# A two-layer decoder on one core: the products of a packed set held together on TensorE, and early work tied to its group's transpose

## The chip, the core and the metric

The kernel runs on one core of one Trainium2 chip. The metric is the time of one execution on the device in microseconds (us); the median of several executions counts. Everything is computed in 32-bit floats. The engines are called as the profile calls them: PE is TensorE's matrix multiplication and PEld its loading of weights, DVE is VectorE, ACT is ScalarE, POOL is GpSimd, and SP is the queue that issues nearly all loads and stores.

## The reference, cut to what matters

The input x is 16 sequences of 128 tokens with 256 features. Two decoder layers follow each other. Each has an attention, a cross stage and a feed-forward stage, and after each stage comes a layer norm of x plus the stage's result:

```python
x = _layernorm(x + _L0_attn_ref(x, ...))   # 16 heads of 64, causal
x = _layernorm(x + _L0_xattn_ref(x, ctx_512, itok, proj_in, proj_out))  # 8 experts, gates
x = _layernorm(x + _L0_ffn_ref(x, ...))    # 2 shared and 16 routed experts, the best 2 taken
x = _layernorm(x + _L1_attn_ref(x, ...))   # 16 heads of 16, a band of 8 to either side
x = _layernorm(x + _L1_xattn_ref(x, ctx_512, ctx_512, ...))  # 16 heads of 16
x = _layernorm(x + _L1_ffn_ref(x, ...))    # 8 experts, scaled by a gate
```

In the second stage the gate of expert e for a token sums `ctx_512` over the places k at which `itok` names e:

```python
onehot = jax.nn.one_hot(ensembles, E, dtype=x.dtype)
gate = jnp.einsum('bks,bkse->bse', weights, onehot)
return jnp.einsum('bsei,bse->bsi', o, gate)
```

So the gates depend on inputs of the kernel alone, and not on x. Neither do the expert weights.

## The kernel before

The 16 sequences form 4 groups of 4, so that a group is 512 tokens. A stage of a group is a Python generator that writes a few instructions and then yields. A planner (`Weaver`, line 193) takes turns between a main chain of stages, a side chain ("dense") and short jobs, by guessed costs and due times. The chains are set at the end (lines 1018 to 1028): first the attention of groups 0 and 1 of layer 0 alone, then that of groups 2 and 3 with dense stages beside it, then the two attentions of layer 1 for all groups with dense stages beside them, and last the dense rest.

This order of writing is not yet the order on the engines. The framework's scheduler takes instructions for each engine by priority, which is the order of writing, among those that it believes ready. So an instruction that was written late but needs little can stand early in its engine's queue. Each engine then runs its own queue strictly in order and waits for semaphores at its head.

**Packed products.** Four kinds of product use only part of the 128x128 array, and are written in sets whose members lie on different parts of it:
- The scores of the attention of layer 0 (line 389): four products for a pair of heads twice, with 64 rows each, from rows 0 and 64.
- Its values (line 432): four products with 64 columns each.
- The scores of the attentions of layer 1 (line 473): two products with 64 rows each and 512 columns of output, one to each of two banks.
- Their values (line 485): four products with 32 columns each.

A fifth kind is the gates' sums (line 751): four products with 32 columns each. Between the members of a set the scheduler may put other products. The other matrix work, projections (292), values' projections (309), hidden layers and the experts' second products (670), uses the whole array. A 32-bit product is two passes in the trace; a transpose (line 51) is one.

**PSUM.** The accumulators are banks of the tags H (projections), M (experts), O (transposes and values), with two buffers each, and S (scores), with one. A projection into H has to wait until DVE or ACT has copied out the one before the last.

**Gates.** `gates0(g)` loads `it` and `cx` into single buffers. Four comparisons on DVE (line 742) give four products `chose`, PE sums each over its partitions, ACT copies the sums, and SP stores them to HBM; then the same for the other four experts. `gates0(g)` is written right after the group's activations were transposed behind its first attention (`tail`, line 951). The transpose consists of eight products on PE and two copies, one on DVE (247) and one on ACT (249). The ACT copy is kept in `transposed_by[g]`. Nothing binds the comparisons to it.

**Expert weights.** The second weights of an expert are needed as seven blocks and their differences. `load_blocks` makes them on POOL when an expert is used first: four subtractions (line 632) and three copies (636), of which only the subtraction of block 4 is bound to the group's transpose. The blocks are stored to HBM and loaded again for the other groups. `together(first, *steps)` is the helper for such a binding: it makes one instruction wait for others.

The sums of the hidden layer's parts (658 to 661), which the experts' second products need, are on DVE.

Of the kernel before, what the change touches and what calls it, by code (L numbers as in the profile page):

```python
# [1 line left out]

# [12 lines left out]
P = 128  # L15
# [12 lines left out]
def kernel(ctx: ExitStack, tc: tile.TileContext, a: dict, out: bass.AP):  # L28
    nc = tc.nc
# [17 lines left out]
    mm = nc.tensor.matmul  # L47

    def transpose(out_, in_):
        n = in_.shape[0]  # L50
        return nc.tensor.transpose(out_, in_, ident[:n, :n])  # L51

    def together(first, *steps):

        for step in steps:
            tc.add_manual_dep(
                first.ins, step.ins.name,
                mybir.DependencyInfo(mybir.DependencyClass.Sync, mybir.DependencyReason.DATA),
                reason="together",
            )  # L60
# [291 lines left out]
    heads0 = {}  # L352

    def attention0(x, g):
        norm = Norm(x)
        norm.bias(bo0)

        def project_quad(g, j):
            wq, wk, wv, wo = first_quads[j] if g == 0 and j < 2 else load_quad(j)
            xT = xTs[g]  # L360
            qT = p2.tile([P, 2, T], F32, tag="qT", name="qT")
            kT = p2.tile([P, 2, T], F32, tag="kT", name="kT")
            for i in range(2):
                c = 2 * j + i
                cols = slice(i * P, (i + 1) * P)
                pq = bank("H")
                project(pq, wq, cols, xT)
                nc.vector.tensor_scalar(
                    qT[:, i, :], pq, bq0[:, c:c + 1], 0.125, ALU.add, ALU.mult
                )  # L370
                pk = bank("H")
                project(pk, wk, cols, xT)
                nc.scalar.activation(kT[:, i, :], pk, AF.Identity, bias=bk0[:, c:c + 1])
                yield 3.44

            v = yield from values(xT, wv, KC)
            heads0[g, j] = qT, kT, v, wo

        def scores(j, b):
            qT, kT, _, _ = heads0[g, j]  # L380
            at = slice(b * P, (b + 1) * P)
            s = ps.tile([P, 2, T], F32, tag="S", name="psS", bufs=1)[:, :, :D].rearrange(
                "p s (i k) -> p s i k", i=2
            )

            for i in range(2):
                for k in range(2):
                    rows = slice(64 * k, 64 * k + 64)
                    mm(  # L389
                        s[:, k, i, :], lhsT=qT[rows, i, at], rhs=kT[rows, i, at],  # L390
                        start=True, stop=True,
                    )
            return softmax(s, causal)

        def output(j, b, zT):
            po = bank("H")[:, :D]
            for i in range(2):
                mm(po, lhsT=zT[:, i, :], rhs=heads0[g, j][3][:, i, :], start=i == 0, stop=i == 1)  # L398
            norm.add(b, po, last=j == 3)

        if (g, 0) not in heads0:
            yield from project_quad(g, 0)
        units = [(j, b) for j in range(4) for b in range(GB)]
        e, eT, zT, at = {}, {}, {}, {}
        for n in range(len(units) + 5):
            if n < 16:
                j, b = units[n]
                e[n] = scores(j, b)
                at["e", n] = weaver.now + 9.0
                yield 0.6  # L410
            m = n - 2
            if m in e:
                yield UNTIL, at["e", m]
                eT[m], _ = weights_T(e.pop(m))
                at["t", m] = weaver.now + 2.5
                yield 0.5
            m = n - 5
            if m in zT:
                yield UNTIL, at["z", m]
                output(*units[m], zT.pop(m))  # L420
                yield 0.86
            m = n - 4
            if m in eT:
                j, b = units[m]
                yield UNTIL, at["t", m]

                pz = bank("O")[:, :D].rearrange("p (c q) -> p c q", c=2)
                got = eT.pop(m)
                for i in range(2):
                    for k in range(2):  # L430
                        h = 2 * i + k
                        mm(  # L432
                            pz[64 * k:64 * k + 64, i, :],
                            lhsT=heads0[g, j][2][:, b, 64 * h:64 * h + 64], rhs=got[:, 2 * k + i, :],
                            start=True, stop=True,
                        )
                zT[m] = p3.tile([P, 2, P], F32, tag="z", name="zT")

                nc.vector.tensor_tensor(
                    zT[m], pz, bv0[:, 2 * j:2 * j + 2].unsqueeze(2).to_broadcast([P, 2, P]), ALU.add  # L440
                )
                at["z", m] = weaver.now + 2.5
                yield 0.6
            if n < 16 and (n < 12 or g + 1 < NG):

                j, b = units[n]
                if b == 0:
                    ahead = project_quad(g, j + 1) if j < 3 else project_quad(g + 1, 0)
                yield next(ahead)
                if b == 3:  # L450
                    assert next(ahead, None) is None
        assert not e and not eT and not zT
        norm.done()


    def attention16(x, qT, kT, v, bv, wo, bo, seen):
# [3 lines left out]
        def scores(b, c):  # L460

            at = slice(b * P, (b + 1) * P)

            kb = p2.tile([P, 4, P], F32, tag="kb", name="kb")
            nc.gpsimd.tensor_tensor(  # L465
                kb, kT[:, c, at].unsqueeze(1).to_broadcast([P, 4, P]),
                hm4.unsqueeze(2).to_broadcast([P, 4, P]), ALU.mult,
            )
            yield UNTIL, weaver.now + 2.0
            s = ps.tile([P, 2, T], F32, tag="S", name="psS", bufs=1)  # L470
            for k in range(2):
                rows = slice(64 * k, 64 * k + 64)
                mm(  # L473
                    s[:, k, :], lhsT=qT[rows, c, at], rhs=kb[rows].rearrange("p h k -> p (h k)"),
                    start=True, stop=True,
                )
            return softmax(s.rearrange("p s (h k) -> p s h k", h=4), seen)

        def weigh(b, c, eT):


            pz = bank("O")[:, :D].rearrange("p (k q) -> p k q", k=2)
            for r in range(4):
                rows = slice(32 * r, 32 * r + 32)
                step = mm(  # L485
                    pz[rows], lhsT=v[:, b, c * P + 32 * r:c * P + 32 * r + 32],
                    rhs=eT[r // 2][0][:, 2 * (r % 2):2 * (r % 2) + 2, :],
                    start=True, stop=True,
                )
                if r == 0:  # L490
                    together(step, eT[1][1])
            if c == 0:
                zT[b] = p3.tile([P, 2, P], F32, tag="z", name="zT16")
            half_z = p2.tile([P, P], F32, tag="hz", name="hz")
            if bv is None:
                nc.scalar.activation(half_z, pz[:, 0, :], AF.Copy, scale=even[:, 0:1])
            else:
                nc.scalar.activation(
                    half_z, pz[:, 0, :], AF.Identity, scale=even[:, 0:1], bias=bv[:, c:c + 1]
                )  # L500
            nc.vector.scalar_tensor_tensor(  # L501
                out=zT[b][:, c, :], in0=pz[:, 1, :], scalar=even[:, 1:2], in1=half_z,
                op0=ALU.mult, op1=ALU.add,
            )
# [8 lines left out]
        e, eT, zT, at = {}, {}, {}, {}  # L513
        for n in range(len(units) + 5):
# [5 lines left out]
            if m in e:  # L520
                yield UNTIL, at["e", m]
                got = e.pop(m)
# [94 lines left out]
    transposed_by = {}  # L617

    def load_blocks(layer, e, g, w):
# [10 lines left out]
        minus = [(4, b01, b00), (5, b11, blocks[:, 4]), (2, blocks[:, 5], b10), (3, b11, b01)]  # L630
        for s, one, two in minus:
            step = nc.gpsimd.tensor_tensor(blocks[:, s], one, two, ALU.subtract)
            if s == 4:
                together(step, *transposed_by[g])
        for s, one in ((0, b00), (1, b10), (6, b11)):
            nc.gpsimd.tensor_copy(blocks[:, s], one)
        held = dp.tile([P, 7, 2 * P], F32, tag=f"wb{layer}", name="wbd", bufs=8)
        nc.gpsimd.dma_start(out=held, in_=t)
        in_hbm[layer, e] = held
# [90 lines left out]
    def gates0(g):  # L730
# [7 lines left out]
        for q in range(2):  # L738
            chose = []
            for r in range(4):  # L740
                t = p4.tile([P, T], F32, tag="cw", name="chose")
                nc.vector.scalar_tensor_tensor(
                    out=t, in0=it.rearrange("p b s -> p (b s)"), scalar=float(4 * q + r), in1=cx,
                    op0=ALU.is_equal, op1=ALU.mult,
                )
                chose.append(t)
            yield UNTIL, weaver.now + 3.5

# [349 lines left out]
```

## Time and profile before

| | |
|---|---|
| three timed executions | 1845.22, 1847.55, 1848.01 us; median 1847.55 |
| the profiled execution's own time | 1843.18 us |
| its span, first to last instruction | 1841.5 us |
| mean granted clock of TensorE | 0.989 |
| DVE | 1017.5 us busy |
| gates' comparisons (742) | 32 of 724 ns, 22.3 us busy |
| differences and copies of blocks (632, 636) on POOL | 64 of 722 to 956 ns, 48 of 434 ns |
| loads of function tables on ACT | 1.283 us each |

The profile is read as follows. A row of a group names line, engine, operation, and the tile written and those read, with the number of times, the busy time and the mean duration. A row of the waits names who waited for whom: microseconds in all, times, and the longest. A row of the timeline begins with start and duration in us, and ends with the engine's idle time before it and what ended it. A row of the windows gives for a stretch of the span its length, the busy time of PE, PEld, DVE, ACT and POOL with the number of instructions, the granted clock of TensorE (1.00 is full), the share of the DMA engines' time and GB/s. Matmuls overlap, and their ends are modelled. So the distance from a start to the next start says more than a duration.

### The profile page before, as it was taken

What the parts mean: (1) busy time and instruction counts of PE and PEld (TensorE: products, weight loads), DVE (VectorE), ACT (ScalarE), POOL (GpSimd) and SP (SyncE); (2) the same over time, 40 slices, a digit from 0 to 9 for tenths busy, and PEclk for the clock granted to TensorE, in tenths of its full rate; (3) what the DMA queues carried; (4) which work ended last, traced back from release to release, by engine and by line L of the source; (5) the groups of instructions that cost most, each with busy time, mean ns of one, the idle gap of its engine ahead of it and who ended that gap; (6) DMA issues with size and microseconds to landing.
All of it is one profiled execution on the core that took longest, in us unless ns stands there. A gap on an engine that the chain in (4) does not pass through costs nothing.

```text
span 1841.5 us, 21636 instructions
## 1 busy us (share of the span) xinstructions
PE 1770.8 (96%) x7620; PEld 1074.5 (58%) x7620; DVE 1017.5 (55%) x1983; ACT 724.2 (39%) x2155; POOL 476.1 (26%) x456
## 2 busy tenths in 40 slices
PE   7999999999999999999999989999998999999997
PEld 4665656666566665565565655544655656556665
DVE  3565566576665244875867644346446455545534
ACT  3444321111123441523404437449466276394121
POOL 4232124310002222413303224253552031230000
PEclk8999999999999999999999999999999999999998
DMA  5032223432321333132233222221322112211321
GB/s 170 27 96 80 69 81 119 145 97 98 121 86 60 99 100 124 64 128 80 75 109 112 66 83 73 92 94 64 126 91 84 63 63 85 85 60 67 136 96 52
DMA packets 73468, 166.70 MB, mean 91 GB/s; under 512 B 7064, under 2 KB 38864, under 8 KB 73360
## 3 DMA queue, kind: packets, MB, share of 16 engines
q1 hardware_dynamic: 70528, 150.17, 24.9%
q0 software_dynamic: 2832, 15.15, 2.0%
q8 instruction: 61, 1.00, 0.2%
q14 instruction: 47, 0.39, 0.1%
HBM read 148.32 MB, written 16.97 MB: 90 GB/s over the span
## 4 chain that ended last, share of the span: by engine, by line
PE 78%; DVE 7%; ACT 7%; DMA 3%; POOL 2%; issue 2%; SPq 0%; POOLq 0%; DVEq 0%; ACTq 0%
PE psH L292 34%; PE psM L670 19%; PE psH L309 4%; PE psO L51 4%; ACT e L333 4%; PE psM L600 3%; PE psH L398 3%; PE psS L473 2%; PE psS L389 2%; PE psO L432 2%; PE psO L485 1%; PE psH L51 1%; DVE nmax L328 1%; ACT L333 1%; DMA wquad<-in_L_attn_W_Q 1%
## 5 line engine op out<-in xcount | busy, mean ns | idle before, releaser
L292 PE MATMUL psH<-xT,we 128*128 128x512 f32 x1024 | 490.7, 601 | 4.7 <-ACT h L934 2.6
L339 POOL TENSOR_TENSOR e<-e,inv 128x512 f32<-128x512 f32 (+1 forms) x128 | 191.3, 1495 | 544.8 <-DVE inv L338 498.2
L292 PEld LDWEIGHTS psH<-xT,we 128*128 128x128 f32 x1024 | 187.8, 191 | 168.1 <-issue 138.8
L333 ACT ACTIVATE e<-e,nmax 128x128 f32<-128x128 f32 x512 | 198.6, 389 | 201.6 <-DVE nmax L328 171.6
L670 PE MATMUL psM<-cm,wb 128*128 128x256 f32 x1024 | 267.1, 385 | 1.3 <-DVE acc L682 1.3
L670 PEld LDWEIGHTS psM<-cm,wb 128*128 128x128 f32 x1024 | 191.8, 191 | 69.5 <-issue 44.5
L682 DVE TENSOR_TENSOR acc<-psM,acc 128x512 f32<-128x512 f32 (+1 forms) x216 | 135.6, 628 | 168.6 <-PE psM L670 167.9
L670 PE MATMUL psM<-h,wb 128*128 128x256 f32 x768 | 202.9, 387 | 0.0
L348 ACT COPY eT<-psO 128x512 f32<-128x512 f32 x192 | 106.8, 587 | 228.3 <-PE psO L51 227.6
L670 PEld LDWEIGHTS psM<-h,wb 128*128 128x128 f32 x768 | 142.9, 192 | 56.1 <-issue 35.5
L934 ACT ACTIVATE h<-psH,b 128x512 f32<-128x512 f32 x128 | 87.3, 688 | 221.1 <-PE psH L292 220.6
L292 PE MATMUL psH<-xT,wquad 128*128 128x512 f32 x256 | 121.1, 615 | 13.0 <-DVE v L313 8.5
L773 DVE SCALAR_TENSOR_TENSOR h<-psH,gt 128x512 f32<-128x512 f32 x128 | 87.6, 686 | 73.2 <-PE psH L292 72.7
L51 PEld LDWEIGHTS psO<-ident,e 128*128 128x128 f32 x768 | 87.7, 141 | 51.2 <-issue 34.7
L292 PE MATMUL psH<-xT,wg 128*128 128x512 f32 x256 | 116.3, 595 | 1.1 <-DVE v L313 1.1
L51 PE MATMUL psO<-ident,e 128*128 128x128 f32 x768 | 112.8, 279 | 1.9 <-DVE zT L501 1.6
L465 POOL TENSOR_TENSOR kb<-kT,hm 128x512 f32<-128x512 f32 x64 | 69.3, 1084 | 153.0 <-PE psS L473 93.4
L333 ACT ACTIVATE e<-psS,nmax 128x128 f32<-128x128 f32 x256 | 89.9, 377 | 33.1 <-DVE nmax L328 26.6
L333 ACT ACTIVATION_READ_ACCUMULATOR e<-e,nmax 128x1 f32 x512 | 95.7, 187 | 0.0
L473 PE MATMUL psS<-kb,qT 64*128 64x512 f32 x256 | 82.0, 644 | 14.1 <-ACT e L333 5.0
L292 PEld LDWEIGHTS psH<-xT,wquad 128*128 128x128 f32 x256 | 47.5, 194 | 67.2 <-issue 47.2
L328 DVE TENSOR_REDUCE nmax<-e 128x4 f32<-128x512 f32 (+1 forms) x96 | 82.5, 859 | 2.0
(179 smaller groups left out, 2277.8 us busy)
## 6 DMA issues: line engine op xcount, KB each, us to landing
wb<-wbd SPq DMA_DIRECT2D x48, 896.0 KB
we<-in_L_xattn_proj_in SPq DMA_DIRECT2D x32, 512.0 KB
we<-in_L_ffn_w SPq DMA_DIRECT2D x32, 512.0 KB
wbd<-wb POOLq DMA_DIRECT2D x16, 896.0 KB, 6.1
gt<-gatesd SPq DMA_DIRECT2D x32, 256.0 KB
cw<-combd SPq DMA_DIRECT2D x64, 128.0 KB
wquad<-in_L_attn_W_Q SPq DMA_DIRECT2D x16, 256.0 KB
wquad<-in_L_attn_W_K SPq DMA_DIRECT2D x16, 256.0 KB
```

What stands on the lines that cost most here:

```text
L51: return nc.tensor.transpose(out_, in_, ident[:n, :n])
L292: mm(pt, lhsT=w[:, c, cols], rhs=xT[:, c, :], start=c == 0, stop=c == KC - 1)
L309: mm(pv[:, i, :], lhsT=xT[:, c, (b + i) * P:(b + i + 1) * P], rhs=w[:, c, :], start=c == 0, stop=c == k - 1,)
L328: nc.vector.tensor_reduce(nmax.rearrange("p (s h) -> p s h", s=2), s, AX.X, ALU.max, negate=True)
L333: nc.scalar.activation(e[:, h, :], s[:, h // (n // 2), h % (n // 2), :], AF.Exp, bias=nmax[:, h:h + 1], accum_out=total[:, h:h + 1],)
L339: nc.gpsimd.tensor_tensor(e, e, inv.unsqueeze(2).to_broadcast([P, n, P]), ALU.mult)
L348: return eT, nc.scalar.copy(eT, pt)
L473: mm(s[:, k, :], lhsT=qT[rows, c, at], rhs=kb[rows].rearrange("p h k -> p (h k)"), start=True, stop=True,)
L670: step = mm(pm[:, s % 2, :], lhsT=blocks[e][:, s, q, :], rhs=parts[e][s][:, q, :], start=q == 0 and s % 2 == 0, stop=q == 1, skip_group_ch ...
L682: nc.vector.tensor_tensor(to, pm[:, :len(slots), :], to, ALU.add)
L773: nc.vector.scalar_tensor_tensor(out=h, in0=ph, scalar=0.0, in1=up[1], op0=ALU.max, op1=ALU.mult)
L934: nc.scalar.activation(h, ph, AF.Gelu, bias=b1[:, 4 * e + c:4 * e + c + 1])
```

## The change

A new helper opens the framework's high-priority context for every product of a set but the first, for the scores and values of both kinds of attention:

```diff
+    def joined(first):
+
+        return nullcontext() if first else tc.high_priority()
...
             for i in range(2):
                 for k in range(2):
                     rows = slice(64 * k, 64 * k + 64)
-                    mm(
-                        s[:, k, i, :], lhsT=qT[rows, i, at], rhs=kT[rows, i, at],
-                        start=True, stop=True,
-                    )
+                    with joined(i == k == 0):
+                        mm(
+                            s[:, k, i, :], lhsT=qT[rows, i, at], rhs=kT[rows, i, at],
+                            start=True, stop=True,
+                        )
```

The same is done with `joined(h == 0)` for the values at line 432, `joined(k == 0)` for the scores at 473 and `joined(r == 0)` for the values at 485. The gates' sums at 751 are left as they are.

All seven instructions that make an expert's blocks, and not one alone, are bound to the group's transpose, and so are the gates' comparisons:

```diff
         for s, one, two in minus:
             step = nc.gpsimd.tensor_tensor(blocks[:, s], one, two, ALU.subtract)
-            if s == 4:
-                together(step, *transposed_by[g])
+            together(step, *transposed_by[g])
         for s, one in ((0, b00), (1, b10), (6, b11)):
-            nc.gpsimd.tensor_copy(blocks[:, s], one)
+            together(nc.gpsimd.tensor_copy(blocks[:, s], one), *transposed_by[g])
...
-                nc.vector.scalar_tensor_tensor(
+                step = nc.vector.scalar_tensor_tensor(
                     out=t, in0=it.rearrange("p b s -> p (b s)"), scalar=float(4 * q + r), in1=cx,
                     op0=ALU.is_equal, op1=ALU.mult,
                 )
+                together(step, *transposed_by[g])
                 chose.append(t)
```

No instruction is moved to another engine: the sums of the hidden layer's parts are on DVE in both kernels, and the differences of the weights' blocks on POOL in both. The number of the program's instructions is the same on every engine but ACT, which has six more loads of function tables.

More of the change, by code (lines that the diff above doesn't have):

```diff
@@ L1 @@
-from contextlib import ExitStack
+from contextlib import ExitStack, nullcontext
 import concourse.bass as bass
@@ L431, in attention0 @@
                         h = 2 * i + k
[L432 to L436, printed above, removed]
+                        with joined(h == 0):
+                            mm(
+                                pz[64 * k:64 * k + 64, i, :],
+                                lhsT=heads0[g, j][2][:, b, 64 * h:64 * h + 64],
+                                rhs=got[:, 2 * k + i, :], start=True, stop=True,
+                            )
                 zT[m] = p3.tile([P, 2, P], F32, tag="z", name="zT")
@@ L472, in scores @@
                 rows = slice(64 * k, 64 * k + 64)
[L473 to L476, printed above, removed]
+                with joined(k == 0):
+                    mm(
+                        s[:, k, :], lhsT=qT[rows, c, at],
+                        rhs=kb[rows].rearrange("p h k -> p (h k)"), start=True, stop=True,
+                    )
             return softmax(s.rearrange("p s (h k) -> p s h k", h=4), seen)
@@ L484, in weigh @@
                 rows = slice(32 * r, 32 * r + 32)
[L485 to L489, printed above, removed]
+                with joined(r == 0):
+                    step = mm(
+                        pz[rows], lhsT=v[:, b, c * P + 32 * r:c * P + 32 * r + 32],
+                        rhs=eT[r // 2][0][:, 2 * (r % 2):2 * (r % 2) + 2, :],
+                        start=True, stop=True,
+                    )
                 if r == 0:
```

## The prediction

> **What bounds the kernel.** Read first: the page's busy shares and its chain.
>
> ```profile
> span 1841.5 us, 21636 instructions
> ...
> PE 1770.8 (96%) x7620; PEld 1074.5 (58%) x7620; DVE 1017.5 (55%) x1983; ACT 724.2 (39%) x2155; POOL 476.1 (26%) x456
> ...
> PE 78%; DVE 7%; ACT 7%; DMA 3%; POOL 2%; issue 2%; SPq 0%; POOLq 0%; DVEq 0%; ACTq 0%
> ```
>
> TensorE is busy for 96% of the span and carries 78% of the chain. So two things count: how long its own work takes, and where it stands still. Second, the waits of PE, longest first.
>
> ```profile
> PE psH L292 <- DVE v L313: 9.6, 2, 8.5
> ...
> PE psS L473 <- ACT e L333: 5.0, 3, 2.3
> ...
> PE psS L473 <- DVE e L323: 2.9, 3, 1.9
> ```
>
> One wait of 8.5 us is by far the longest; the rest is many small ones. Third, the timeline of DVE and of PE around it, and the clock there.
>
> ```profile
> 24.76 0.69 DVE L742 SCALAR_TENSOR_TENSOR chose<-it,cx 128x512 f32<-128x512 int32 x1 [12.23 <-DMA cx<-in_ctx]
> 25.37 0.68 DVE L313 COPY v<-psH 128x512 f32<-128x512 f32 x1
> ...
> 16.84 0.71 PE L389 MATMUL psS<-kT,qT 64*128 64x128 f32 x8
> 26.11 6.57 PE L292 MATMUL psH<-xT,wquad 128*128 128x512 f32 x8 [8.55 <-DVE v L313]
> 32.61 0.71 PE L389 MATMUL psS<-kT,qT 64*128 64x128 f32 x8
> ...
> 26.10:32.60 6.50, 6.49 (x8) 2.52 (x8) 4.61 (x8) 1.65 (x8) 3.05 (x5) 0.55 0.10 41
> ```
>
> A gate of group 0 (L742), whose sums PE makes only after 130 us, heads DVE's queue and waits 12.2 us for the load of cx. Behind it stands the copy that frees PE's bank. After the stop the granted clock (third number from the end of the last row) is 0.55. Fourth, the packed products, each beside the start of what follows it, whole and broken.
>
> ```profile
> 65.01 0.71 PE L389 MATMUL psS<-kT,qT 64*128 64x128 f32 x8
> 65.66 0.66 PE L51 MATMUL psO<-ident,e 128*128 128x128 f32 x4
> ...
> 74.28 0.49 PE L389 MATMUL psS<-kT,qT 64*128 64x128 f32 x4
> 74.70 0.55 PE L51 MATMUL psH<-ident,x 128*128 128x128 f32 x3
> ...
> 1117.95 1.12 PE L473 MATMUL psS<-kb,qT 64*128 64x512 f32 x2
> 1119.00 3.70 PE L292 MATMUL psH<-xT,wg 128*128 128x512 f32 x8
> ...
> 1514.81 1.13 PE L473 MATMUL psS<-kb,qT 64*128 64x512 f32 x4
> 1515.87 1.99 PE L670 MATMUL psM<-cm,wb 128*128 128x256 f32 x8
> ```
>
> Each product is two passes. Half a set of scores takes 0.42 us, the whole 0.65; half a pair at L473 takes 1.05 us, the whole 1.06, so the second half rides almost free. Single starts show what a visit to packed work adds outside: passes of 128x256 start 216 ns apart, 309 ahead of a packed one and 320 for the first behind it, so 93 + 104 = 197 ns. Last, how full two stages are.
>
> ```profile
> 200.00:600.00 400.00, 398.86 (x1752) 250.81 (x1752) 245.44 (x496) 86.26 (x283) 74.50 (x89) 1.00 0.30 99
> ...
> 1597.80:1655.10 57.30, 53.99 (x224) 28.89 (x224) 27.19 (x43) 51.71 (x151) 19.30 (x13) 1.00 0.17 61
> ```
>
> From 200 to 600 us PE hardly stops (398.9 of 400). In the last attention of 16 channels a head, ACT (fifth number) works 51.7 of 57.3 us.
>
> **The start.** The new order of the built program has no gate among DVE's first 130 instructions. PE's first projection with the second weights then follows its scores at about 17.5 us. The bank is free: the value products began at about 13.4 us, so the copy ends near 16. The load is there too: every issue on SP waits for the eighth before it, and the one that waits for the last part of the second weights (it, group 0) was through by 16.3 us. Gain: the stop, 8.6 us (17.5 to 26.1), plus the slow clock: 6.50 us from start to next start, against 8 x 0.429 + 0.09 = 3.53, so 3.0. Together 11.6.
>
> Here a rule can be weighed. The Trainium skill ("TensorE: Matmul & The Clock Gate", Part 1) says that an idle window of about 3.4 us halves PE's clock until some 3.4 us of work. By that the tail is 3.4 x 0.5 = 1.7 us and the gain 10.3; the row says 3.0, and I take the row.
>
> What is late next? The first transposes need DVE's minimum and maximum (0.69 + 0.69), a table load (1.28), four exponentials with their read-outs (4 x 0.58), 0.18 and POOL's 1.04: 6.2 us after the scores, near 23.7; PE reaches them after two more projections and score sets, near 26. POOL matters: before, four instructions of the first weights' differences (one of 0.96 us, three copies of 0.43) head its queue and wait for a load until 27.2. They are tied to the transpose too and leave; otherwise 27.2 + 2.2 + 1.04 = 30.5 would cost back some 4 us. The weights are first multiplied after 200 us, so building all seven blocks later (5.1 us from 130) is hidden. No DMA of either step moves early: SP's order is the same for the first 43 issues, and differs by a few places of five loads later. A second stop, at 150.6 us (1.2 us, PE on x L267 with a gate of group 1 waiting 3.9 us ahead on DVE), goes for the same reason.
>
> **The products.** I counted unbroken stretches in both built orders; those of before agree with the trace.
> - Scores L389: 45 whole, 4 of three, 26 of two, 12 single become 63 whole, 2 of two. At 0.645, 0.638, 0.421, 0.415 us: 47.5 to 41.5, so 6.0; and 22 visits fewer x 0.197 = 4.3. Sum 10.3.
> - Values L432: 65 stretches become 62, five broken ones go: 0.9 + 0.6 = 1.5.
> - Scores L473: 55 pairs, 15 halves, one of three become 64 pairs: 75.5 to 67.8, so 7.7; 7 visits 1.4. Sum 9.1.
> - Values L485: unchanged.
> - Gate sums L751 are not joined, and get worse: 12 stretches become 15 (7 single, 2 of two, 3 of three, 3 whole at 0.98 to 1.00 us): 2.9 + 0.6 = 3.5 lost.
>
> Of these, L389 and L432 lie before 660 us, where nothing but PE is the limit: 11.8 taken whole. L473 lies from 740 us, and here a rule speaks against the change. The skill's "TensorEngine Tiling" (PSUM Bottleneck) says that packing speeds the array and not the emptying of PSUM. A pair makes 128x1024 scores, for which DVE needs 1.21 + 1.21 us and ACT 8 x 0.58 = 4.6 us with 90% of its time gone: by the rule PE only waits longer, 0; by the rows above 9.1. Dense products fill PE in between, so I take half, 4.6. The gates' 3.5 count in full. Products: 11.8 + 4.6 - 3.5 = 12.9.
>
> **What it adds.** Each group's gates now wait for ACT's copy, four in a row on DVE. Behind them stand the dense hidden layers' products (L773, L879) or value copies (L313), whose banks PE needs. Bounds a group: 0 when the copy is early, 4 x 0.69 = 2.8 when all is exposed. Two banks hide one or two dense units (1.7 us each); I take 0.5 a group, 2.0. The order also has six more table loads of 1.28 us on ACT: 0 to 7.7; ACT is 39% busy, I take 1.0. Reordering could also gain here, for which I have no reason.
>
> Sum: 11.6 + 1.2 + 12.9 - 2.0 - 1.0 = 22.7. The profiled execution took 1843.2 us (span 1841.5), so 1820.5. The three timed ones lie 2 to 5 us higher, median 1847.55: there 1824.9, say 1825.
>
> **Rivals.**
> - Start only: what L389 to L473 save turns into waits, of which PE had some 60 us after 700 us. 1847.6 - 12.8 + 3 = 1838. For it: ACT's 90%. Against: the full PE from 200 to 600. Chance 0.20.
> - All of it: L473 counts in full and the added waits cost nothing: 12.8 + 17.4 = 30, 1817. Chance 0.10.
> - Slower: the tied gate heads DVE's queue while ACT's copy stands behind a unit's exponentials. Price: 4.6 + 1.28 for a table, + 2.8 for the four gates = 8.7 us a group, 35 in all, against 24.7 won: 1858. It decides from 6.2 us a group on average. Against: in the new order the gates stand where DVE's neighbours also await these transposes. Chance 0.04.
> - No difference: the waits of other stages are drawn anew and eat all of it, near 1846. Chance 0.04. That the joining fails is ruled out by the order (63 of 64 sets whole).
> - The forecast, near 1825: 0.62.
>
> A measurement of this kernel tells about 0.2% (3.7 us) from no change. Faster by more: 0.62 + 0.20 + 0.10 = 0.92; within: 0.04; slower: 0.04. The range, 1812 to 1841, takes in both faster rivals, with some 4 us of other waits either way.
>
> **What would show it.** Right: no PE gap over 1 us before 60 us, clock 1.0 at 20 us, the second score set near 21 and not 32.6 us; L389 in stretches of x8, L473 of x4; groups at L389 by 660 us ending some 22 us earlier. Wrong: a wait of PE on DVE after each group's transposes of 5 us or more, or a sum of PE waits after 700 us that grows by more than 9.

## The result, and the profile after

The changed kernel takes 1819.85 us (median of 4, 1817.60 to 1822.47); the kernel before, on the same chip, takes 1847.15 us (4, 1845.22 to 1848.01). The ratio is 0.9854, with a 95% interval of 0.9837 to 0.9871: faster by 27.3 us. The forecast was 1825.0 us with a range of 1812 to 1841. A second measurement of the same changed kernel (below, e8) gave 1817.94 us, 29.4 us under the kernel before of that measurement.

The profiled execution of the changed kernel took 1822.47 us, 20.7 less than that of before (1843.18). The profiled one of before had been 4.0 us under its median, and this one is 2.6 us over its own. So the traces of these two show 6.6 us less than the medians do; the trace of e8 shows 25.4.

All line numbers that follow for the changed kernel are its own: 394 is the 389 of before, 438 the 432, 480 the 473, 493 the 485, 759 the 751 (gates' sums), 749 the 742 (gates' comparisons), 640 and 643 the 632 and 636 (blocks), 343 the 339 (POOL's scaling of the exponentials), 296 the 292 and 313 the 309. First, from the page of the changed kernel, the span, the busy time of each engine, and the chain.

```profile
span 1820.8 us, 21658 instructions
...
PE 1757.9 (97%) x7620; PEld 1073.8 (59%) x7620; DVE 1016.4 (56%) x1983; ACT 731.5 (40%) x2161; POOL 476.0 (26%) x456
...
PE 78%; ACT 9%; DVE 8%; POOL 2%; issue 2%; DMA 1%; POOLq 0%; DVEq 0%; SPq 0%; ACTq 0%
```

Nothing was removed from the program, yet PE is busy for 12.9 us less with the same 7620 instructions. It is as much the bound as before (97%, 78% of the chain). Second, the waits of PE in the changed kernel, longest first (microseconds in all, times, longest).

```profile
PE psO L51 <- DVE zT L509: 5.4, 3, 3.4
PE psO L493 <- ACT eT L352: 5.2, 8, 1.8
...
PE psS L480 <- ACT e L337: 4.5, 4, 1.9
```

The wait of 8.5 us for DVE's copy of v has left the list. What heads it now are waits in the second layer's attentions, of up to 3.4 us each. Third, the timeline of PE in the changed kernel at the start, and at one pair of the second layer's scores.

```profile
14.03 3.62 PE L313 MATMUL psH<-wquad,xT 128*128 128x256 f32 x16
17.58 0.71 PE L394 MATMUL psS<-kT,qT 64*128 64x128 f32 x8
18.22 3.70 PE L296 MATMUL psH<-xT,wquad 128*128 128x512 f32 x8
21.85 0.71 PE L394 MATMUL psS<-kT,qT 64*128 64x128 f32 x8
...
1103.38 1.13 PE L480 MATMUL psS<-kb,qT 64*128 64x512 f32 x4
1104.44 3.70 PE L296 MATMUL psH<-xT,wg 128*128 128x512 f32 x8
```

And the window of that first projection in the changed kernel (length, busy time of PE, PEld, DVE, ACT and POOL, granted clock, DMA share, GB/s).

```profile
18.20:21.80 3.60, 3.60 (x10) 1.44 (x8) 2.45 (x5) 1.65 (x8) 0.07 (x1) 1.00 1.09 348
```

Each row begins where the one above it ends: there is no stop, the clock is 1.00 where it had been 0.55, and the second set of scores begins at 21.85 us and not at 32.61. Both kinds of scores stand in whole sets here, and over the whole trace as the prediction had counted them: 63 whole sets and two halves at line 394, 64 whole pairs at line 480.

**Where the time went.** Two measures follow the gain through the traces. The first is the lead: the time at which ACT copies a group's transposed activations in the profiled execution of before, minus the same in another kernel. The second splits the span. PE's own work is an estimate: the sum of the distances from start to start when nothing holds PE, which are 429, 216 and 109 ns for passes of 512, 256 and 128 columns, plus the 93 and 104 ns around packed products. What is left between PE's first and last start is excess: waits and slow clock. (Some 10 us of each span lie outside these two.)

| profiled execution | lead at 50 us | 130 | 227 | 404 | 664 | 1074 | 1241 | 1327 | 1448 | end | PE's own work | excess to 60 us | excess after |
|---|---|---|---|---|---|---|---|---|---|---|---|---|---|
| before | | | | | | | | | | | 1740.0 | 13.9 | 77.2 |
| after | 10.5 | 11.6 | 11.7 | 14.2 | 17.1 | 14.6 | 13.9 | 14.6 | 19.3 | 20.7 | 1724.2 | 3.2 | 83.0 |
| e8, after again | 11.1 | 12.1 | 11.6 | 14.1 | 17.0 | 16.1 | 15.5 | 17.4 | 23.8 | 25.4 | 1723.8 | 2.7 | 79.0 |
| e3, both ties | 11.0 | 11.0 | 5.2 | 5.3 | 5.2 | 5.9 | 4.0 | 4.3 | 2.9 | 3.0 | 1741.8 | 3.1 | 83.2 |
| e4, sets joined | -0.7 | 0.3 | 4.0 | 6.5 | 9.4 | 6.2 | 6.0 | 9.7 | 14.4 | 15.7 | 1721.1 | 14.4 | 79.9 |
| e5, ties and sets of layer 0 | 10.6 | 11.5 | 11.4 | 13.7 | 16.6 | 19.0 | 18.9 | 15.6 | 15.6 | 15.5 | 1733.9 | 3.2 | 78.5 |
| e6, ties and sets of layer 1 | 10.8 | 10.8 | 4.3 | 4.3 | 4.3 | 1.8 | 0.9 | 1.5 | 6.3 | 7.7 | 1730.8 | 3.4 | 89.3 |
| e9, e3 and later blocks | 11.4 | 10.6 | 9.9 | 8.8 | 8.7 | 11.0 | 11.8 | 19.3 | 17.7 | 17.6 | 1740.9 | 2.9 | 69.7 |

The changed kernel's own work is 15.8 to 16.2 us less, the start gives 10.7 to 11.2, and the rest of the excess grows by 1.8 to 5.8.

### The profile page after: what moved, and what is told of

It reads as the page before. It is cut to its first block, busy times and chain, and to the rows that moved or that the text cites. A ratio compares the mean times of both kernels' runs of the same rounds, so it can differ in the third digit from the quotient of the medians.

```text
span 1820.8 us, 21658 instructions
## 1 busy us (share of the span) xinstructions
PE 1757.9 (97%) x7620; PEld 1073.8 (59%) x7620; DVE 1016.4 (56%) x1983; ACT 731.5 (40%) x2161; POOL 476.0 (26%) x456
## 4 chain that ended last, share of the span: by engine, by line
PE 78%; ACT 9%; DVE 8%; POOL 2%; issue 2%; DMA 1%; POOLq 0%; DVEq 0%; SPq 0%; ACTq 0%
PE psH L296 34%; PE psM L677 18%; ACT e L337 5%; PE psH L313 4%; PE psO L51 4%; PE psM L608 3%; PE psH L403 3%; PE psS L394 2%; PE psO L438 2%; PE psS L480 2%; PE psO L493 1%; PE psH L51 1%; ACT L337 1%; ACT L942 1%; PE psH L517 1%
## 5 line engine op out<-in xcount | busy, mean ns | idle before, releaser
L296 PE MATMUL psH<-xT,wquad 128*128 128x512 f32 x256 | 117.3, 601 | 1.2 <-DMA wquad<-in_L_attn_W_Q 0.7
L480 PE MATMUL psS<-kb,qT 64*128 64x512 f32 x256 | 73.2, 648 | 13.4 <-issue 4.7
```

The source lines that it names most:

```text
L296: mm(pt, lhsT=w[:, c, cols], rhs=xT[:, c, :], start=c == 0, stop=c == KC - 1)
L480: mm(s[:, k, :], lhsT=qT[rows, c, at], rhs=kb[rows].rearrange("p h k -> p (h k)"), start=True, stop=True,)
```

## The experiments

My theory was that of the prediction: both ties together free the start and nothing else; whole sets save PE's own work, of which nearly all counts in layer 0 and about half in layer 1. The rivals: one tie is enough; the ties only move the stop; the sets' saving turns into waits in layer 1, or counts in full. Three measurements were made, each with the kernel before beside it: 1846.25 us for e1 to e4, 1847.33 for e5 to e8, 1846.69 for e9 to e12.

### One tie, the other, and both (e1, e2, e3)

e1 is the kernel before with the comparisons tied, e2 with the weights tied, e3 with both:

```diff
# e1 and e3
-                nc.vector.scalar_tensor_tensor(
+                step = nc.vector.scalar_tensor_tensor(
...
+                together(step, *transposed_by[g])
# e2 and e3
-            if s == 4:
-                together(step, *transposed_by[g])
+            together(step, *transposed_by[g])
...
-            nc.gpsimd.tensor_copy(blocks[:, s], one)
+            together(nc.gpsimd.tensor_copy(blocks[:, s], one), *transposed_by[g])
```

> The kernel before, with the gates' comparisons alone tied to the transpose. Theory (both ties are needed for the whole start): the comparisons leave the head of DVE's queue, so the stop of 8.6 us on PE and the slow clock behind it go, but four instructions of the first weights still head POOL's queue until 29.5 us, and PE then waits some 4 us for the first transposes: 4 to 7 us faster than before, and in the trace a wait of PE at line 51 on POOL near 26 us. Rival (the weights' tie does nothing): 10 to 12 us faster, no such wait.

> The kernel before, with the blocks of the weights alone tied to the transpose. Theory: DVE's stop stays, and what POOL did under it was hidden, so no difference: within 2 us of before, the 8.5 us wait still there. Rival (POOL took part in the stop): 3 us faster or more.

> The kernel before with both ties and no joined products. Theory: the start alone, 8.6 + 3.0 us, and 1.2 at 150 us, less 1 to 2 for gates made in a row: 10 to 12 us faster. Rival (the ties cost elsewhere what they win): under 8 us. A second rival (the joined products are worth little, the ties nearly all): 20 us or more.

Measured: e1 1845.24 us, ratio 0.9997 (0.9986 to 1.0008); e2 1846.35 us, 0.9996 (0.9984 to 1.0009); e3 1840.65 us, 0.9968 (0.9954 to 0.9982). So neither tie alone gives anything, and both together give 5.6 us. For e2 my theory had this; for e1 it had 4 to 7 us, and failed. Why e1 does not gain the whole stop is in its timeline, PE first and POOL behind it.

```profile
29.93 1.11 PE L51 MATMUL psO<-ident,e 128*128 128x128 f32 x4 [3.80 <-POOL e L339]
...
27.13 0.72 POOL L632 TENSOR_TENSOR wb<-raw 128x256 f32<-128x256 f32 x1 [9.37 <-DMA raw<-in_L_xattn_proj_out]
27.80 1.08 POOL L636 COPY wb<-raw 128x256 f32<-128x256 f32 x3
28.85 2.03 POOL L339 TENSOR_TENSOR e<-e,inv 128x512 f32<-128x512 f32 x2
```

With DVE free, the first transposes wait for POOL, whose queue is headed by the first weights' blocks: they wait for their load until 27.13, make PE wait 3.80 us, and the scaling (L339) comes behind them. This is the loss of "some 4 us" that the prediction names for the case without the weights' tie. A slow clock comes on top (0.50 granted from 29.9 to 33.4 us), so that at 50 us e1 leads by 5.0 us and e3 by 11.0. At 130 us e1 still leads by 4.9, but at 227 us it is 0.9 us behind: it loses 5.8 us at a second place.

e3 has no such wait at the start; its lead at 50 us is 11.0, as forecast. But it holds only until 130 us, and at 227 us it is 5.2: the same 5.8 us are lost. My theory wanted 10 to 12 us at the end and was refuted in that; the rival that named less than 8 was right. The timeline of e3 shows the place, PE first and then POOL.

```profile
133.05 1.12 PE L51 MATMUL psO<-ident,e 128*128 128x128 f32 x4 [3.62 <-POOL e L339]
...
136.99 4.56 PE L292 MATMUL psH<-xT,wquad 128*128 128x512 f32 x8
...
129.44 1.53 POOL L632 TENSOR_TENSOR wb<-raw 128x256 f32<-128x256 f32 x2 [3.27 <-DMA raw<-in_L_xattn_proj_out]
130.94 0.71 POOL L632 TENSOR_TENSOR wb<-raw,wb 128x256 f32<-128x256 f32 x1
131.61 0.39 POOL L635 COPY wb<-raw 128x256 f32<-128x256 f32 x1
131.96 1.03 POOL L339 TENSOR_TENSOR e<-e,inv 128x512 f32<-128x512 f32 x1
```

It is the same pattern once more, 100 us later. The blocks of the second expert stand ahead of a scaling in POOL's queue and wait 3.27 us for their load; the scaling comes at 131.96, PE has waited 3.62 us for it, and the eight passes at 136.99 run at a lower clock (0.50 granted from 133 to 137 us, and 4.56 us for them and not 3.70).

Which tie brings this order? The POOL queue of e1 at the same place:

```profile
132.95 2.40 POOL L632 TENSOR_TENSOR wb<-raw 128x256 f32<-128x256 f32 x2 [3.28 <-DMA raw<-in_L_xattn_proj_out]
...
138.18 1.03 POOL L339 TENSOR_TENSOR e<-e,inv 128x512 f32<-128x512 f32 x1
```

And that of the kernel before:

```profile
133.92 1.05 POOL L339 TENSOR_TENSOR e<-e,inv 128x512 f32<-128x512 f32 x1
137.29 1.42 POOL L632 TENSOR_TENSOR wb<-raw 128x256 f32<-128x256 f32 x2 [2.32 <-DMA raw<-in_L_xattn_proj_out]
```

In the kernel before, the scaling stands ahead of the second expert's blocks, which wait for their load there too. In e1 it stands behind them, as in e3, and PE waits 3.4 us for it, though in e1 the weights are tied no more than in the kernel before. In e2, in which all of them are tied, PE has no such wait, and the lead stays (0.2 us at 130, 0.1 at 227). So the order that costs here comes with the gates' tie and not with that of the weights. Why the scheduler makes it was not tested.

### The joined sets (e4, e5, e6)

e4 is the changed kernel without the ties. e5 is the changed kernel with only layer 0's sets joined, e6 with only layer 1's (`joined(True)` gives no product priority):

```diff
# e5: lines 480 and 493
-                with joined(k == 0):
+                with joined(True):
...
-                with joined(r == 0):
+                with joined(True):
# e6: lines 394 and 438
-                    with joined(i == k == 0):
+                    with joined(True):
...
-                        with joined(h == 0):
+                        with joined(True):
```

> The kernel before with joined products and no ties. Theory: products shorten PE's work by 17 us, of which those before 660 us count whole and those at the scores of layer 1 by half: 12 to 16 us faster, the 8.5 us stop still there. Rival (packed time turns into waits): under 6 us. Second rival (all of it counts): 17 us or more.

> The changed kernel without joining in the two attentions of layer 1; layer 0's products joined, both ties. Theory: start 11 to 12 us, joined products of layer 0 some 10 us less 3 for the gates' sums, which break up: 17 to 20 us faster than before, some 5 us behind the changed kernel. Rival (layer 1 gains nothing): as fast as the changed kernel, within 2 us.

> The changed kernel without joining in the attention of layer 0; layer 1's products joined, both ties. Theory (half of 9.1 us counts): start 11 to 12 us and 4 to 6 more, 15 to 18 us faster than before. Rival (all waits in the end): 10 to 12. Second rival (nothing is lost): 20 or more.

Measured: e4 1826.65 us, 0.9898 (0.9880 to 0.9917), 19.6 us less; e5 1826.99 us, 0.9893 (0.9876 to 0.9910), 20.3 less; e6 1832.88 us, 0.9925 (0.9909 to 0.9940), 14.5 less. e4 gave more than the 12 to 16 us of my theory, and the rival "17 or more" was right. e5 ended 0.3 us above the range of the theory and e6 0.5 below, but e5 is 9.1 us behind the changed kernel measured beside it, not the "some 5" that I expected: layer 1's sets are worth more.

By medians the parts add up: 5.6 for the ties (e3), 20.3 - 5.6 = 14.7 for layer 0's sets, 14.5 - 5.6 = 8.9 for layer 1's. The sum is 29.2, and the whole change measured 27.3 and 29.4. The 14.7 of layer 0 are two things. PE's own work is 7.9 us less in e5 than in e3. And the loss of lead from 130 to 227 us is gone (11.5 to 11.4 in e5, 11.0 to 5.2 in e3): with the sets joined, POOL's scaling stands ahead of the second expert's blocks, here in the changed kernel:

```profile
125.55 1.05 POOL L343 TENSOR_TENSOR e<-e,inv 128x512 f32<-128x512 f32 x1
128.72 1.86 POOL L640 TENSOR_TENSOR wb<-raw 128x256 f32<-128x256 f32 x2 [2.12 <-DMA raw<-in_L_xattn_proj_out]
```

e6, in which layer 0's sets are broken, loses it too (10.8 to 4.3). So part of the ties' gain only comes with the sets: without them they give 5.6 us, and with them 29.4 - 19.6 = 9.8 (e8 against e4). The intervals of these medians are too wide to tell 5.6 from 9.8; it is the traces that show the loss and where it goes.

Layer 1's sets reduce PE's own work by 10.1 us (1733.9 in e5, 1723.8 in e8), and 29.4 - 20.3 = 9.1 of that comes out at the end by medians (7.0 with the first measurement of the changed kernel), 9.9 by the traces of e8 and e5. On the way part becomes waits: from 664 to 1074 us the lead of e5 rises from 16.6 to 19.0, and that of e8 falls from 17.0 to 16.1. It comes back from 1241 to 1448 us. Which order of the stages makes it come back, I did not test.

### The gates' sums in whole sets (e7), and the changed kernel again (e8)

Of the five kinds of packed product, the gates' sums were left broken. In e7 they are joined too, and the first of a set waits for the last comparison:

```diff
+                chosen = step
...
-                mm(
-                    pg[32 * r:32 * r + 32, :], lhsT=ones[:, :32], rhs=chose[r],
-                    start=True, stop=True,
-                )
+                with joined(r == 0):
+                    step = mm(
+                        pg[32 * r:32 * r + 32, :], lhsT=ones[:, :32], rhs=chose[r],
+                        start=True, stop=True,
+                    )
+                if r == 0:
+                    together(step, chosen)
```

> The changed kernel, in which the first gate sum of a set also waits for the last comparison and the other three have high priority, so that all eight sets are whole (15 stretches become 8). Theory: 7 stretches less at about 0.98 + 0.2 us are 8 us less work on PE; the wait costs up to 2 us at two sets; 4 to 8 us faster than the changed kernel. Rival (the broken sums stood where PE would have waited): within 2 us of the changed kernel.

> The changed kernel itself, beside the other three on one chip: about 27 us faster than before, as measured; 21 would say that the first measurement was high.

Measured: e7 1821.50 us, 0.9859 (0.9840 to 0.9878); e8 1817.94 us, 0.9849 (0.9830 to 0.9868). So my theory, 4 to 8 us faster, was wrong: whole sums give nothing that can be told (by medians e7 is 3.6 us slower than e8), although PE's own work falls by another 10.3 us, to 1713.5. The timeline of PE in e7, at the first group's gates:

```profile
123.57 1.94 PE L761 MATMUL psH<-chose,ones 128*32 128x512 f32 x8 [1.90 <-DVE chose L749]
125.44 2.65 PE L313 MATMUL psH<-wquad,xT 128*128 128x256 f32 x8
...
134.61 1.11 PE L51 MATMUL psO<-ident,e 128*128 128x128 f32 x4 [3.22 <-POOL e L343]
```

The same place in the changed kernel:

```profile
120.28 2.18 PE L759 MATMUL psH<-chose,ones 128*32 128x512 f32 x4 [0.30 <-DVE chose L749]
...
122.76 1.05 PE L759 MATMUL psH<-chose,ones 128*32 128x512 f32 x2
...
127.71 1.75 PE L759 MATMUL psH<-chose,ones 128*32 128x512 f32 x6
```

The broken sums follow the comparisons as these come, and fill time in which PE waits in e7. The whole ones take less of PE, but PE waits 1.90 us for the comparisons and, behind, 3.22 us for POOL; after the first of these waits the clock is low, too (0.50 granted from 123.5 to 125.4 us). The lead of e7 falls from 11.5 to 7.6 us between 130 and 227. It gains later (26.7 at the end of its trace, whose execution was the shortest of its four, 1816.46 us).

### Later blocks (e9 to e12)

If the blocks on POOL are what takes the lead at 130 us, then making them later must give it back. In e9 (e3) and e10 (the changed kernel) and e11 (e7), the blocks of every expert but the first wait for the last hidden layer of the expert before it:

```diff
-            together(step, *transposed_by[g])
+            together(step, *(behind or transposed_by[g]))
...
-            together(nc.gpsimd.tensor_copy(blocks[:, s], one), *transposed_by[g])
+            together(nc.gpsimd.tensor_copy(blocks[:, s], one), *(behind or transposed_by[g]))
...
-                    hidden(h[e][:, c, :], up[e], e, c)
+                    ended = [hidden(h[e][:, c, :], up[e], e, c)]
```

In e12, on top of e10, the first expert's blocks wait too, for ACT's copy of the gates' last sums:

```diff
-            nc.scalar.copy(sums, pg)
+            summed = nc.scalar.copy(sums, pg)
...
+        transposed_by[g] = [summed]
```

> Both ties without joined products, and the blocks of every expert but the first wait for the last hidden layer of the expert before. In the run with both ties alone, PE waited 3.6 us for POOL's scaling of weights (line 339) at 133 us, which stood behind the second expert's blocks and their load, and then ran at a slow clock: 11.0 us ahead of the kernel before at 130 us, 5.2 at 227. Theory (those blocks in POOL's queue are the cause): that wait goes, the lead at 227 us is 9 to 11, and the time 9 to 12 us below the kernel before. Rival (the gates in a row on DVE are the cause): the wait stays 3 us or more, though on DVE's or ACT's chain, and the time is 4 to 7 us below before.

> The changed kernel with the same later blocks. In the changed kernel POOL never held PE there. Theory: 0 to 2 us faster than the changed kernel, which lies near 1818 to 1820. Rival (POOL's blocks at that place still cost by slowing DVE): 3 us or more.

> Gates' sums kept whole and the later blocks. With whole sums alone PE waited 3.2 us on POOL and 1.9 on the comparisons at group 0. Theory: the first goes with its slow clock, so 4 to 6 us faster than with whole sums alone (1821.5), near 1816, and 2 to 4 us faster than the changed kernel. Rival: the order changes elsewhere eat it, within 2 us of 1820.

> As with the later blocks on the changed kernel, and the first expert's blocks wait for the gates' second sums, so that POOL does not work while DVE compares. In the changed kernel the four comparisons took 4.25 us in a row beside POOL's blocks, against 2.7 without. Theory (POOL slows DVE): each comparison of group 0 is back to about 0.69 us, and the time is 1 to 3 us below the changed kernel. Rival (the comparisons are long for another reason): they stay at about 1 us, and the time does not move.

Measured: e9 1826.36 us, 0.9895 (0.9881 to 0.9910), 20.3 less than before; e10 1816.24 us, 0.9836 (0.9821 to 0.9851); e11 1819.58 us, 0.9854 (0.9840 to 0.9867); e12 1813.14 us, 0.9820 (0.9805 to 0.9835).

e9 settles the place: its wait for POOL near 133 us is gone, and the lead goes from 10.6 to 9.9 us where e3 loses 5.8. But it gains 14.7 us over e3 (20.3 less 5.6), and of that I had foreseen some 5. Most of the other is one step of lead between 1241 and 1327 us (11.8 to 19.3), where layer 1's first experts begin and the blocks of its later ones are no longer released all at once. That step's mechanism was not tested by itself; stages can also trade dense work there, so it stays open.

e10 has the same step (12.1 to 19.6), but it leads less than e8 from 227 us on (10.9 at 227, 14.4 at 664), and both traces end at a lead of 25.4. Its ratio and that of e8 cannot be told apart, so neither its theory nor its rival is decided by the time. e11 cannot be told from e7: at the first group PE still waits 1.9 us for the comparisons, and 1.7 us for POOL, a wait that I had expected to go. Of my numbers for these, the 1816 us for e11 was a miss, and so were those for e9 (9 to 12 us below the kernel before) and e12 (1 to 3 us below the changed kernel): both gained more.

e12 is the fastest kernel of this study, 33.5 us under before. Its interval lies below that of the first measurement of the changed kernel, overlaps that of e8 at its edge and that of e10, measured beside it, by half. So by time alone it is only likely that e12 is faster than e10; the trace shows a cause. The timeline of the changed kernel at the first group's gates, DVE first and then POOL:

```profile
119.04 4.25 DVE L749 SCALAR_TENSOR_TENSOR chose<-it,cx 128x512 f32<-128x512 int32 x4
...
120.77 1.17 POOL L640 TENSOR_TENSOR wb<-raw,wb 128x256 f32<-128x256 f32 x1
121.89 0.85 POOL L643 COPY wb<-raw 128x256 f32<-128x256 f32 x1
...
123.82 0.73 POOL L643 COPY wb<-raw 128x256 f32<-128x256 f32 x2
```

The same comparisons in e12, where POOL does nothing beside them until 121.95 us:

```profile
118.61 2.49 DVE L750 SCALAR_TENSOR_TENSOR chose<-it,cx 128x512 f32<-128x512 int32 x4
...
121.95 1.04 POOL L343 TENSOR_TENSOR e<-e,inv 128x512 f32<-128x512 f32 x1 [7.41 <-DVE inv L342]
```

Four comparisons take 4.25 us beside POOL's blocks and 2.49 us without them. POOL's copy takes 0.85 us while DVE compares, and two take 0.73 us just after it has ended. The two engines slow each other in these instructions, but not in all. Over the traces of all 14 profiled kernels a comparison takes 0.69 us in the median with POOL idle and 1.19 us where POOL computes beside it for over 80% of its time. For the addition of the mask to the scores (line 323 of before), of whose inputs one is in PSUM, and for the maximum (328), which has one input, both medians are 0.68 to 0.69 us. A comparison reads two tiles from SBUF. In e12 the lead rises from 12.1 to 13.8 us between 130 and 227, where it falls from 11.3 to 10.9 in e10.

## Why the prediction was right, point by point

- **The start (11.6).** Right in size and mechanism. The excess until 60 us falls by 10.7 and 11.2 in two traces, and the clock is full. Of the two sizes that the prediction weighs for the slow clock (1.7 and 3.0 us), the trace of before bears out the larger: 0.50 was granted from 26.1 to 31.0 us. e1 and e2 show that both ties are needed here (leads of 5.0, 0.2 and 11.0 us at 50 us in e1, e2 and e3). The loss without the weights' tie was put at some 4 us: the wait of e1 is 3.80, but with the slow clock behind it 6.0 us are lost.
- **The second stop (1.2).** The wait of 1.2 us near 150 us is not among the waits of PE from 105 to 235 us in the changed kernel. What it gave was not measured apart from the gates, which lie in the same stretch.
- **"Building all seven blocks later is hidden".** Right for the changed kernel as far as no wait of PE for POOL appears there, but in part by luck. The step counted 5.1 us of POOL's time, and not what stands behind blocks in POOL's queue: in e1, e3 and e6 the gates' tie puts the second expert's blocks, with the wait for their load, ahead of a scaling, and 5.8 to 6.5 us of lead are lost. Only the order of the joined kernel puts the scaling first, and nothing in the prediction says so. Asking who is queued behind, as the prediction did for the start, would have shown the risk at 130 us too. Nor are the first expert's blocks quite hidden: they slow the comparisons, as e12 shows (next point).
- **Gates in a row (0.5 a group, at most 2.8).** The bound was too low: the first group's four comparisons took 4.25 us, not 2.8, because POOL made blocks beside them. A wait of PE on DVE of 5 us or more did not appear. Over the first group's gates the changed kernel gained 0.1 us (traces of e8: -0.5) where the joined sets alone gained 3.7 (e4). So, by difference, about 3.6 to 4.2 us went to these gates with their broken sums, in one group and not spread over four: from 227 to 664 us both kernels gain the same 5.4. Some 2 us of it come from POOL's blocks: e12, with the same broken sums, gains 1.7 there where e10 loses 0.4.
- **Layer 0's products (11.8, less 3.5 for the gates' sums).** Right: 8.3 was forecast, and PE's own work in e5 is 7.9 less than in e3.
- **Scores of layer 1 (9.1, of which half).** This is the term that was mis-sized. The work fell by 10.1, with the values joined as well, and by medians 7.0 to 9.1 of that counts, not 4.6; in e6 8.9. The rule that packing only makes PE wait longer in these stages was weighed and half believed. The waits did appear, between 664 and 1074 us, but most of it was won back later. The added waits after 700 us were small: 46.3 us in all in the trace of before, 48.7 after, 47.7 in e8, far from the 9 us more that would have spoken against the forecast.
- **Six more table loads (1.0).** PE's waits for ACT changed little (for the exponentials 5.0 to 4.5 us, for the copies of their transposes 3.9 to 5.2). The loads' cost was not measured alone.
- **The sum.** 22.7 was forecast and the traces show 20.7 and 25.4; by medians it is 27.3 and 29.4. The difference between the medians and 22.7 is 4.6 to 6.7, and 2.4 to 4.5 of it is layer 1's other half. The rest is within what single executions differ by (1817.60 to 1822.47 for the same kernel). Two errors partly cancel in the sum, which is luck. One sign was not met: by 660 us the groups were to end some 22 us earlier, which left under 1 us for all that follows. The lead at 664 us is 17.1 and 17.0, and 3.6 and 8.4 us come after it. The first group's gates cost more than forecast, and layer 1's sets gave more. The rival "all of it" (1817), which was given a chance of 0.10, lies nearer to both medians (1819.85 and 1817.94) than the forecast; "start only" (1838) and "slower" (1858) are excluded by every run of the changed kernel.

## What to carry to other kernels

Where the matrix engine is full, keep the members of a packed set together: each visit cost 197 ns here, and a lone half of a pair with 512 columns took as long as the whole (1.05 and 1.06 us). Work that needs only inputs was put by this scheduler at the head of in-order queues. So tie such work to the moment at which it is wanted, on every queue that it heads (one tie alone gave nothing), and then read the new order of every queue: the gates' tie on DVE's queue changed POOL's, 100 us later, and cost half of what both ties had won in e3. Where dense work can move into the waits of a stage with several limits, discount a gain there less: 7.0 to 9.1 of 10.1 us came out here.

## What was not expected of the hardware

- DVE and POOL slowed each other by 1.6 to 2.3 times: a comparison of 128x512 took 1.06 us beside POOL's blocks and 0.62 without (4.25 and 2.49 for four); a subtraction of 128x256 on POOL took 1.17 us beside the comparisons and 0.71 in e3; a copy 0.85 and 0.37. It was not so for DVE's work that reads only one tile from SBUF (0.68 to 0.69 us beside POOL and without).
- A stop of PE of under 4 us can be followed by a slow stretch as well: eight passes took 4.56 and not 3.70 us some 4 us after the 3.62 us wait of e3. In e7 the granted clock was 0.50 even after a wait of 1.90 us; in e11, after a wait as long at the same place, it was 1.00 (123.4 to 126.2 us).
